# The split of the next job's weights, given a place 300 instructions earlier in the scheduler's order

## The chip, the cores and the metric

The kernel runs on one core of one Trainium2 chip. The metric is the device time of one execution in microseconds (us), the median of several executions. The engines are named as the profile names them: PE is the matrix engine (PEld its weight loads), DVE the vector engine, ACT the scalar engine, POOL the gather and scatter engine, SP the engine that only issues transfers. Each engine works through its own list of instructions in order. An instruction whose input is not there yet holds up everything behind it on its engine.

## The reference, cut to what matters

One layer of a graph network on 1250 nodes of width 1024 with 20000 edges, sorted by target, of 8 types. The part that the change touches is the relational convolution and the projections beside it:

```python
xn = _layernorm(x)
out = xn @ root + bias
for r in range(8):
    mask = (edge_type == r)
    sums = segment_sum(xn[src] * mask[:, None], dst)
    cnt = segment_sum(mask, dst)
    out = out + (sums / maximum(cnt, 1)[:, None]) @ weight[r]
z = concatenate([out, xn]) @ w_gate + b_gate
h = tanh(out) * z + xn * (1 - z)
```

Beside it stand a linear attention over all nodes (projections `w_q`, `w_kv`, `w_out`) and, after both, a gated feed-forward layer whose operands are rounded to a 4-bit grid in blocks of 16. All data is float32.

## The kernel before

**Products first, messages after.** The kernel turns the order of the convolution round: it first multiplies all nodes by the weight of each type (`y_d`, 8 x 1250 rows, in two halves of 512 columns) and then adds up, for each target, the rows of `y_d` that its edges name, each times 1/count. Three products are made in plain float32 in the front part of the program (`plain`). The remaining 18 are **jobs** of the function `product`, numbered 0 to 17 here: jobs 0 to 4 are the rest of the first half (types 3 to 7), jobs 5 to 12 the second half of all 8 types, job 13 the q, k and v projections (384 columns), jobs 14 and 15 the root product, jobs 16 and 17 the half of the gate that acts on `xn`.

**A job.** A job multiplies ten blocks of 128 nodes by one 1024 x 512 weight matrix, in float32 made of three faster products of split operands. The nodes' split operands (`xH`, `xL`, `xD`) are resident. The weights are split by `limb(job, k)`, lines 476 to 491, for each of the eight slices k of 128 rows: SP loads the slice (`raw`, three buffers), DVE masks it (`h`, L487, two buffers), ACT copies the mask as `wH` (L488), DVE makes `wL` (L489) and `wD` (L490). That is one load, one ACT and three DVE instructions. The three results live in the pool `wl`, which has 26 places: 24 for the eight slices of the running job and two over. Hence the split of the next job can't go far ahead; most of it has to wait until the last block of the running job has used a slice. Therefore `product` calls `more(k)` only within its last piece: after the last block's matmuls of slice k (L529 to L531) it traces the next job's slice k + 1.

A job has nine pieces: blocks 0 and 1 together (48 matmuls), then one block at a time (24 matmuls each). After a piece, ACT and DVE take the sums out of PSUM (L537, L538, and L545 where there is a bias line), and ACT issues the store (L546). After that comes the job's share of other work, called `beside`: in jobs 0 to 4 the rounding of the feed-forward weights (`ffn_rows`), in jobs 5 to 12 about 20 messages each, in jobs 13 to 17 28 messages each.

**A message** is a tile of 128 edges, for one half of the columns: there are 157 for each half, 314 in all. POOL gathers 128 rows of `y_d` into `msg` (L444, four buffers); two messages later DVE makes a 0/1 matrix `sel` (L453), ACT `hi` (L455) and DVE the remainder in `msg` (L457), PE multiplies twice (L460, L461) into one of two PSUM tiles, ACT copies the sums out (L462) and issues their store to `seg_d` (L463). The messages of the second half (numbers 157 to 313 here) can't start before job 12 has stored its last block, since they gather from what jobs 5 to 12 write. 140 of them are spread over jobs 13 to 17; the last 17 come after the jobs.

**After the jobs** follow the sums for the attention (`mix_sums`, `mix_pairs`), the closing of segments that cross tiles (`open_segments`, lines 764 to 779, the second call after the last message), the numerators of the attention for blocks 0 to 4 (`mix_num`) with the transposes of the feed-forward weights between them (`ffn_weight`, L157), and then ten blocks of the gate, the output and the feed-forward layer, which PE paces.

**What sets the order.** The program is traced from top to bottom. The tile framework then schedules it on a simulated machine: whenever an engine is free there, it takes, of the instructions whose inputs and buffers are ready, the one with the lowest number. The number is the place in tracing order. The order found that way is fixed in the program, and the chip's engines follow it whatever happens there. `tc.high_priority(n)` lowers the numbers of what is traced inside it by n, and the numbering goes on as before when it is left.

Of the kernel before, what the change touches and what calls it, by code (L numbers as in the profile page):

```python
# [26 lines left out]
H, DH = 8, 16  # L27
FIRST = 5
LAG = 2
EARLY = 140  # L30
PLAIN = 3
TOP = -4096
# [6 lines left out]
def block_rows(b):  # L39
    return slice(b * BR, min((b + 1) * BR, N))  # L40


def rows_of(b):
    return min(BR, N - b * BR)
# [3 lines left out]
def gps_layer(ctx: ExitStack, tc: tile.TileContext, x, src, dst, et, w_rel, w_root, bias,  # L48
# [393 lines left out]
    def gather(nh, t):  # L442
        msg = em.tile([128, HD], F32, name="msg")
        gathered_last[0] = G.indirect_dma_start(  # L444
            out=msg[:, :], out_offset=None, in_=y_d[nh][:, :],
            in_offset=bass.IndirectOffsetOnAxis(ap=key[:, t:t + 1], axis=0)).ins
        return lambda: segments(nh, t, msg)
# [28 lines left out]
    def limb(job, k):  # L476
        raw = rawp.tile([128, HD], F32, name="raw")
        if job is QKV:
            V.memset(raw[:, 384:], 0.0)
            nc.sync.dma_start(raw[:, :128], w_q[k * 128:(k + 1) * 128, :])  # L480
            nc.sync.dma_start(raw[:, 128:384], w_kv[k * 128:(k + 1) * 128, :])
            V.tensor_scalar(raw[:, :384], raw[:, :384], gm[:, k:k + 1], None, op0=ALU.mult)
        else:
            nc.sync.dma_start(raw, job[0][k * 128:(k + 1) * 128, :])
        h = topp.tile([128, HD], F32, name="h")
        Wh, Wl, Wd = (wl.tile([128, HD], F32R, name=f"w{c}", tag="w") for c in "HLD")
        V.tensor_scalar(h.bitcast(I32), raw.bitcast(I32), TOP, None, op0=ALU.bitwise_and)  # L487
        S.copy(Wh, h)  # L488
        V.tensor_tensor(Wl, raw, h, ALU.subtract)  # L489
        V.scalar_tensor_tensor(Wd, Wl.bitcast(F32), -1.0 / LOW, h, op0=ALU.mult, op1=ALU.add)  # L490
        return Wh, Wl, Wd

    psum_pools(ctx, sg=2)
    with ExitStack() as main:
# [5 lines left out]
        jobs = [(w_rel[r][:, cols[nh]], y_d[nh][r * N:(r + 1) * N, :], None)  # L500
                for nh, r in [(0, r) for r in range(PLAIN, R)] + [(1, r) for r in range(R)]]
        jobs += [QKV] + [(w[:, cols[nh]], d[:, cols[nh]], v[cols[nh]])
                         for w, d, v in ((w_root, root_d, bias), (w_gate[D:2 * D, :], gx_d, b_gate)) for nh in range(2)]
        held_of = [[] for _ in jobs]
        anchor = [None]

        def product(i, beside, from_=0, to_=9):


            job, held = jobs[i], held_of[i]  # L510
            _, dest, line = job
            n = dest.shape[1]
            if line is not None:
                rows_line = bias_p.tile([128, HD], F32, name="line")
                nc.sync.dma_start(rows_line, line[None, :].to_broadcast([128, HD]))

            def more(k):
                if i + 1 < len(jobs) and k < KC:
                    held_of[i + 1].append(limb(jobs[i + 1], k))

            def piece(blocks, last):
                ab = [[psum["ab"].tile([128, HD], F32, name="ab") for _ in range(2)] for _ in blocks]
                if last:
                    more(0)
                for k in range(KC):
                    Wh, Wl, Wd = held[k]
                    for (pa, pb), b in zip(ab, blocks):
                        ns, p = block_rows(b), rows_of(b)
                        T.matmul(pa[:p, :n], xH[:, k, ns], Wh[:, :n], start=(k == 0), stop=False)  # L529
                        T.matmul(pa[:p, :n], xL[:, k, ns], Wl[:, :n], start=False, stop=(k == KC - 1))  # L530
                        T.matmul(pb[:p, :n], xD[:, k, ns], Wd[:, :n], start=(k == 0), stop=(k == KC - 1))  # L531
                    if last:
                        more(k + 1)
                for (pa, pb), b in zip(ab, blocks):
                    p = rows_of(b)
                    yt = yp.tile([BR, HD], F32, name="yt")[:p]
                    S.mul(yt[:, :n], pa[:p, :n], 1.0 + LOW)  # L537
                    made = V.scalar_tensor_tensor(yt[:, :n], pb[:p, :n], -LOW, yt[:, :n], op0=ALU.mult, op1=ALU.add)  # L538
                    if i == R - PLAIN - 2:
                        anchor[0] = made.ins  # L540
                    if job is QKV:
                        V.tensor_scalar(yt[:, :128], yt[:, :128], rms[:p, b, 1:2], None, op0=ALU.mult)
                        V.tensor_scalar(yt[:, 128:n], yt[:, 128:n], rms[:p, b, 0:1], None, op0=ALU.mult)
                    if line is not None:
                        V.tensor_tensor(yt, yt, rows_line[:p], ALU.add)  # L545
                    S.dma_start(dest[block_rows(b), :], yt[:, :n])  # L546

            groups = [(0, 1)] + [(b,) for b in range(2, NB)]
            done = 0
            for j, g in enumerate(groups):  # L550
                piece(g, j == len(groups) - 1)
                while done < len(beside) and done * (to_ - from_) < len(beside) * (j + 1 - from_):
                    beside[done]()
                    done += 1
# [32 lines left out]
        def message(nh, t):  # L587

            if t < ST:
                waiting.append(gather(nh, t))  # L590
            if t >= LAG:
                waiting.pop(0)()

        def messages(nh, t0, t1):
            return [lambda t=t: message(nh, t) for t in range(t0, t1)]


        tiles = messages(0, 0, ST + LAG)
        for i in range(R):
            product(n0 + i, share(tiles, i, R))  # L600

        tiles = messages(1, 0, EARLY)
        for i in range(5):
# [63 lines left out]
    with ExitStack() as late:  # L667
# [26 lines left out]
        def mix_pairs(b):  # L694
            if b == 0:
                bd_ps.append(mm_tile())
            ps, n = bd_ps[0], rows_of(b)
            kks = []
            for c in range(4):
                kk = pb.tile([BR, 2, DH, DH], F32, name="kk")[:n]  # L700
                ck = kv[:n, b, c * 32:c * 32 + 32].rearrange("p (h i) -> p h i", h=2)
                cv = kv[:n, b, 128 + c * 32:128 + c * 32 + 32].rearrange("p (h e) -> p h e", h=2)
                V.tensor_tensor(kk, ck[:, :, None, :].to_broadcast([n, 2, DH, DH]),
                                cv[:, :, :, None].to_broadcast([n, 2, DH, DH]), ALU.mult)
                kks.append(kk.rearrange("p h e i -> p (h e i)"))
            for c, kk in enumerate(kks):
                T.matmul(ps[32 * c:32 * c + 32], kv[:n, b, 32 * c:32 * c + 32], kk,
                         start=(b == 0), stop=(b == NB - 1))
            if b == NB - 1:
                V.scalar_tensor_tensor(  # L710
                    bd.rearrange("p (h x) -> p h x", h=2), ps.rearrange("p (h x) -> p h x", h=2), 0.5,
                    mask2[:, :, None].to_broadcast([128, 2, 256]), op0=ALU.mult, op1=ALU.mult)
# [77 lines left out]
        rest += [lambda b=b: mix_pairs(b) for b in range(NB)]  # L790
        done = EARLY
        for i, p in enumerate(rest):
            p()
            while done < ST + LAG and (done - EARLY) * len(rest) < (i + 1) * (ST + LAG - EARLY):
                message(1, done)
# [137 lines left out]
```

## Time and profile before

| | us |
|---|---|
| median of 3 runs | 2024.85 (2014.6 to 2028.79) |
| the profiled execution | 2014.05 |
| its span in the trace | 2012.3 |
| front part, to the first matmul of job 0 | 298.2 |
| jobs 0 to 4 | 298.2 to 583.8 |
| jobs 5 to 12 | 583.8 to 1124.8 |
| jobs 13 to 17 | 1124.8 to 1502.1 |
| after the jobs, to the first transpose of the first output block | 1502.1 to 1652.1 |
| ten output blocks | 1652.1 to 2012.3 |

The limits of the stages are starts of instructions in the timeline: the first L529 of a job, and the first L157 on `u`. A job's matmul of 512 columns starts 0.23 us after the one before it when PE runs at full clock, although each is shown as 0.39 us long: matmuls overlap. So a block of 24 takes 5.6 us, and a gap is best read as the time between two starts beyond 0.23 us. Summed so over jobs 0 to 17, PE lost 81 us, of which 51 us in jobs 13 to 17. By job, start, length and time lost of the last ones:

| job | starts at | length | messages multiplied in it | lost | of it in the first piece | in the last piece |
|---|---|---|---|---|---|---|
| 10 | 919.3 | 66.9 | 20 | 1.9 | 1.6 | 0.0 |
| 11 | 986.2 | 67.9 | 20 | 2.9 | 2.1 | 0.0 |
| 12 | 1054.1 | 70.7 | 20 | 5.7 | 3.5 | 0.0 |
| 13 | 1124.8 | 55.4 | 17 | 4.5 | 0.0 | 0.1 |
| 14 | 1180.3 | 89.9 | 34 | 18.4 | 11.3 | 6.3 |
| 15 | 1270.2 | 80.5 | 28 | 11.8 | 3.0 | 8.1 |
| 16 | 1350.7 | 79.7 | 28 | 11.1 | 2.4 | 7.8 |
| 17 | 1430.5 | 71.9 | 24 | 5.5 | 3.3 | 0.2 |

### The profile page before, as it was taken

How to read it: one execution, taken by the hardware profiler on the slowest of the kernel's cores; microseconds unless marked ns; L12 is line 12 of the kernel's file. 1: busy time of each engine (PE TensorE's matmuls, PEld its weight loads, DVE VectorE, ACT ScalarE, POOL GpSimd, SP SyncE). 2: the span in 40 equal slices, each digit the busy share in tenths (PEclk: the TensorE clock that was granted, in tenths of full speed). 3: DMA queues.
4: the chain of work that ended last, by engine and by line, in shares of the span. 5: the costliest groups of instructions: out<-in, count | busy, mean ns of one | idle time of the engine just before them, and what ended most of it. 6: DMA issues, size and time to landing. Idle time of an engine off the chain costs nothing. (4 is left out here: it accounts for less than half of the span.)

```text
span 2012.3 us, 24046 instructions
## 1 busy us (share of the span) xinstructions
PE 1889.7 (94%) x7828; PEld 1281.7 (64%) x7828; DVE 1315.7 (65%) x2940; ACT 755.3 (38%) x1307; POOL 614.1 (31%) x588
## 2 busy tenths in 40 slices
PE   6999999999999999999999989999897689999998
PEld 3465547777777777777777877667663244454544
DVE  6989936776644565456545666666655677777665
ACT  6211321121224454545454455555553223132311
POOL 2012478885012333333332234333243310010000
PEclk8999999999999999999999989889998759999999
DMA  6245324444336677766776687787689532122100
GB/s 211 75 137 142 102 58 132 121 121 126 117 118 213 223 227 227 229 229 222 226 228 202 205 254 253 240 253 241 214 264 320 199 101 84 63 84 69 37 21 29
DMA packets 158868, 332.76 MB, mean 165 GB/s; under 512 B 26974, under 2 KB 35844, under 8 KB 158742
## 3 DMA queue, kind: packets, MB, share of 16 engines
q0 software_dynamic: 39168, 110.63, 21.1%
q10 hardware_dynamic: 76570, 141.23, 18.9%
q1 hardware_dynamic: 43004, 79.36, 12.6%
q8 instruction: 62, 1.02, 0.2%
q14 instruction: 64, 0.52, 0.1%
HBM read 184.42 MB, written 146.53 MB: 164 GB/s over the span
## 5 line engine op out<-in xcount | busy, mean ns | idle before, releaser
L529 PE MATMUL ab<-wH,xH 128*128 128x512 f32 (+2 forms) x1440 | 569.2, 395 | 2.3 <-ACT wH L488 2.3
L531 PE MATMUL ab<-wD,xD 128*128 128x512 f32 (+2 forms) x1440 | 562.9, 395 | 3.8 <-DVE wD L490 3.1
L530 PE MATMUL ab<-wL,xL 128*128 128x512 f32 (+2 forms) x1440 | 565.3, 393 | 0.0
L444 POOL DMA_INDIRECT msg<-y_d,key x314 | 329.5, 1049 | 677.4 <-PE sm L461 328.3
L457 DVE SCALAR_TENSOR_TENSOR msg<-msg,weight,hi 128x512 fp32r<-128x512 f32 x314 | 234.0, 749 | 145.3 <-ACT hi L455 142.5
L531 PEld LDWEIGHTS ab<-wD,xD 128*128 128x128 f32 (+1 forms) x1440 | 268.6, 187 | 76.9 <-DVE wD L490 12.8
L529 PEld LDWEIGHTS ab<-wH,xH 128*128 128x128 f32 (+1 forms) x1440 | 270.2, 188 | 64.8 <-ACT wH L488 4.1
L530 PEld LDWEIGHTS ab<-wL,xL 128*128 128x128 f32 (+1 forms) x1440 | 270.1, 188 | 64.4 <-DVE wL L489 0.4
L455 ACT ACTIVATE hi<-msg,weight 128x512 fp32r<-128x512 f32 x314 | 222.4, 721 | 87.9 <-DMA msg<-y_d,key 29.4
L462 ACT COPY seg<-sm 128x512 f32<-128x512 f32 x314 | 181.8, 584 | 193.0 <-PE sm L461 150.3
L388 PE MATMUL mm<-wt,xnT 128*128 128x512 f32 (+1 forms) x480 | 225.6, 611 | 5.1 <-DMA wt<-in_L_gnn_weight_dram 5.1
L370 POOL DMA_INDIRECT sort_d<-pay,row x160 | 208.5, 1303 | 60.2 <-issue 48.4
L537 ACT ACTIVATE yt<-ab 128x512 f32<-128x512 f32 (+2 forms) x180 | 106.0, 592 | 319.8 <-PE ab L530 308.0
L538 DVE SCALAR_TENSOR_TENSOR yt<-ab,yt 128x512 f32<-128x512 f32 (+2 forms) x180 | 121.5, 680 | 144.8 <-ACT yt L537 143.9
L460 PE MATMUL sm<-hi,sel 128*128 128x512 f32 x314 | 133.3, 429 | 33.4 <-ACT hi L455 28.7
L453 DVE TENSOR_SCALAR sel<-iota_n,last_row 128x128 fp32r<-128x128 f32 x314 | 89.0, 286 | 104.5 <-PE sm L461 104.2
L461 PE MATMUL sm<-msg,sel 128*128 128x512 f32 x314 | 136.0, 434 | 21.7 <-DVE msg L457 21.5
L849 PE MATMUL mm<-wg,uT 128*128 128x512 f32 (+1 forms) x320 | 141.7, 596 | 1.5 <-DVE mr L122 1.0
L388 PEld LDWEIGHTS mm<-wt,xnT 128*128 128x128 f32 (+1 forms) x480 | 85.7, 190 | 90.0 <-issue 82.5
L488 ACT CAST wH<-h 128x512 fp32r<-128x512 f32 x144 | 88.5, 621 | 126.2 <-DVE h L487 119.0
L489 DVE TENSOR_TENSOR wL<-raw,h 128x512 fp32r<-128x512 f32 x144 | 98.1, 682 | 31.9 <-PE mm L388 31.9
L849 PEld LDWEIGHTS mm<-wg,uT 128*128 128x128 f32 (+1 forms) x320 | 59.5, 189 | 75.2 <-issue 70.4
(267 smaller groups left out, 2042.8 us busy)
## 6 DMA issues: line engine op xcount, KB each, us to landing
seg_d<-seg ACTq DMA_DIRECT2D x314, 256.0 KB
y_d<-yt ACTq DMA_DIRECT2D x144, 256.0 KB
raw<-in_L_gnn_weight_dram SPq DMA_DIRECT2D x104, 256.0 KB
db<-in_dst_dram POOLq DMA_DIRECT2D x32, 305.2 KB, 3.9
xt<-in_x_dram SPq DMA_DIRECT2D x18, 512.0 KB
msg<-y_d,key POOLq DMA_INDIRECT x314, 4.7
lb<-lo_d POOLq DMA_DIRECT2D x32, 156.2 KB, 4.0
root_d<-yt ACTq DMA_DIRECT2D x18, 256.0 KB
```

What stands on the lines that cost most here:

```text
L370: st = G.indirect_dma_start(out=sort_d[:, :], out_offset=bass.IndirectOffsetOnAxis(ap=row[:, t:t + 1], axis=0), in_=pay[:, t, :], in_offse ...
L388: T.matmul(ps[:n], xnT[:, k, block_rows(b)], held[k], start=(k == 0), stop=(k == KC - 1))
L444: gathered_last[0] = G.indirect_dma_start(out=msg[:, :], out_offset=None, in_=y_d[nh][:, :], in_offset=bass.IndirectOffsetOnAxis(ap=key[:, ...
L455: S.mul(hi, msg, weight[:, t:t + 1])
L457: V.scalar_tensor_tensor(lo, msg, weight[:, t:t + 1], hi.bitcast(F32), op0=ALU.mult, op1=ALU.subtract)
L460: T.matmul(ps, sel, hi, start=True, stop=False)
L461: T.matmul(ps, sel, lo, start=False, stop=True)
L462: S.copy(seg, ps)
L529: T.matmul(pa[:p, :n], xH[:, k, ns], Wh[:, :n], start=(k == 0), stop=False)
L530: T.matmul(pa[:p, :n], xL[:, k, ns], Wl[:, :n], start=False, stop=(k == KC - 1))
L531: T.matmul(pb[:p, :n], xD[:, k, ns], Wd[:, :n], start=(k == 0), stop=(k == KC - 1))
L849: T.matmul(ps[:n], uT[:, k, :n], wg[:, k, cs], start=(k == 0), stop=(k == KC - 1))
```

## The change

The instructions that `limb` traces from within `more` get numbers lower by 300. Nothing is added or removed: the same loads, splits, matmuls and messages are there, on the same engines, with the same buffers. Only the order in which the scheduler chooses among ready instructions is different. The first job's split, traced outside `more`, keeps its numbers.

```diff
 LAG = 2
+AHEAD = 300
 EARLY = 140
...
             def more(k):
                 if i + 1 < len(jobs) and k < KC:
-                    held_of[i + 1].append(limb(jobs[i + 1], k))
+                    with tc.high_priority(AHEAD):
+                        held_of[i + 1].append(limb(jobs[i + 1], k))
```

## The prediction

> **What bounds the kernel now.** I read the page first, then the table of stretches, then single engines in order of time. The page says PE is busy nearly throughout, with one dip:
>
> ```profile
> PE 1889.7 (94%) x7828; PEld 1281.7 (64%) x7828; DVE 1315.7 (65%) x2940; ACT 755.3 (38%) x1307; POOL 614.1 (31%) x588
> ...
> PE   6999999999999999999999989999897689999998
> ...
> PEclk8999999999999999999999989889998759999999
> ```
>
> Each slice is 50.3 us; the dip in slices 30 to 32 is the stretch after the jobs. The split of the weights lies in slices 6 to 28, where PE shows 8 or 9: what can be gained there is at most the 81 us lost between starts. The table of stretches, at the end of job 15, shows where such loss sits:
>
> ```profile
> core 0: us, PE busy (x) PEld busy (x) DVE busy (x) ACT busy (x) POOL busy (x), PEclk, DMA share, GB/s
> ...
> 1341.00:1351.00 10.00, 5.69 (x10) 2.62 (x11) 6.08 (x13) 5.30 (x11) 3.78 (x4) 0.68 0.77 248
> 1351.00:1365.00 14.00, 13.87 (x52) 10.21 (x52) 12.41 (x24) 7.03 (x12) 1.47 (x1) 0.87 0.65 200
> 1365.00:1400.00 35.00, 35.00 (x150) 27.48 (x149) 21.60 (x42) 18.94 (x33) 15.08 (x14) 1.00 0.80 261
> ```
>
> For 10 us PE does only 10 matmuls, and neither DVE nor ACT is full. PE in order of time says why:
>
> ```profile
> 1342.83 0.49 PE L461 MATMUL sm<-msg,sel 128*128 128x512 f32 x1 [0.81 <-DVE msg L457]
> 1344.62 0.79 PE L460 MATMUL sm<-hi,sel 128*128 128x512 f32 x1 [1.30 <-ACT hi L455]
> 1345.41 0.79 PE L461 MATMUL sm<-msg,sel 128*128 128x512 f32 x1
> 1347.50 0.80 PE L460 MATMUL sm<-hi,sel 128*128 128x512 f32 x1 [1.30 <-ACT hi L455]
> ...
> 1350.13 0.80 PE L461 MATMUL sm<-msg,sel 128*128 128x512 f32 x1 [0.62 <-DVE msg L457]
> 1350.72 0.63 PE L529 MATMUL ab<-wH,xH 128*128 128x512 f32 x1
> ```
>
> The last block's matmuls are done at 1340.5, and the next job's first matmul (L529) starts at 1350.72. Between them PE has nothing but messages, each waiting for its own ACT and DVE steps. The next job's weights are not split: DVE's first L489 of the new job starts at 1350.0 though its place was free long before. From there DVE splits at a slice per 1.54 us (L490 at 1357.73, 1359.28, 1360.82, 1362.36), and now the messages stand still, as POOL shows:
>
> ```profile
> 1351.20 1.47 POOL L444 DMA_INDIRECT msg<-y_d,key  x1 [0.90 <-PE sm L461]
> 1367.27 0.94 POOL L444 DMA_INDIRECT msg<-y_d,key  x1 [14.60 <-PE ab L531]
> ```
>
> So a boundary has two parts in series: about 10 us of messages without product, then 14 us of splitting without messages. In jobs 5 to 11 the first part is missing: L490 starts 0.5 us into the last piece, and only 1.6 to 2.1 us are lost in the next first piece, before an L461 whose DVE step stands behind the splits.
>
> The difference is the backlog. Gather 157 starts at 1136.8, 12 us into job 13, which multiplies 17 of its 28 messages. At 3.1 messages per piece the 11 missing ones are 3.5 pieces of older numbers, and in the scheduler's order they come before the split.
>
> **What the Trainium skill says.** "TensorE: Matmul & The Clock Gate", section "What's actually happening", has PE's clock halved after an idle window of about 3.4 us and restored after a busy one. The trace agrees: from 1350.72 to 1354.6 the starts are 0.43 us apart, later 0.23. A stall thus costs some 2 us beyond itself. "DMA: Bandwidth & Descriptors", section "Issuing engines are not separate DMA queues", says that transfers from all queues interleave on the same 16 engines: gathers slow down beside bulk loads. That bears on the stretch after the jobs; there the DMA share is 0.98 to 1.03 from 1500 to 1540, and an ACT step of a message waits 7.2 us for its gather.
>
> **The change, part by part.** I add up against the profiled execution's 2014.05 us (span 2012.3 and 1.75 around it). Every instruction keeps its length: L487 0.42, L488 0.62, L489 and L490 0.68 us, and SP's loads 0.33 each to issue. All five move together.
>
> *How far 300 reaches.* A one-block piece of jobs 13 to 17 traces 24 matmuls, 3 or 4 output instructions and 3.1 messages of 8, some 53 instructions: 300 are 5.7 pieces. The split passes messages of about pieces 3 to 7 and remains behind older ones. In jobs 5 to 12 (45 per piece) 300 are 6.7 pieces.
>
> *Jobs 0 to 4.* The split passes the rounding of the feed-forward weights on DVE and its loads on SP. Job 1's first piece takes 14.8 us against 11.1 in jobs 2 and 4, job 3's 11.5: I take **-4**, ends 0 and -5. The rounded weights are read only after 1502, so their delay is covered.
>
> *Jobs 5 to 12.* The split is on time already. What PE waits for is a message behind the split, and that isn't cured by putting the split further ahead. I take **0**, ends -12 (1.5 us at each of 8 boundaries) and +12.
>
> *Jobs 13 to 17.* Removable is what was lost at the boundary beyond the 1.6 us of jobs 5 to 11. Into 14: 11.3 - 1.6 = 9.7. Into 15: 6.3 + 3.0 - 1.6 = 7.7. Into 16: 8.1 + 2.4 - 1.6 = 8.9. Into 17: 7.8 + 3.3 - 1.6 = 9.5. But a job without stalls is shorter, so fewer messages fit beside it. The backlog grows from 11 by about 5 per job, to 16, 21 and 26, or 3.5, 5, 7 and 8 pieces. At the last two boundaries part of it is older than 300 instructions, so the split waits again. I take the first two in full, the last two by half: 9.7 + 7.7 + 4.4 + 4.7 = **-26.5**, ends -15 and -34. With jobs 0 to 4 the jobs end 30 us earlier.
>
> *Messages.* What waits behind the split on DVE, ACT and SP is the messages, and for them POOL and PE. Each boundary stops them for about 14 us, as it did before (16 us by POOL's gaps), so the stop isn't new. But they have less time: before, 365 us from gather 157 to the end of the jobs, less 4 x 16 = 301 for 131 messages, 2.30 us each. Now 365 - 26.5 - 56 = 282 us, 123 messages. Eight more are left for the stretch after the jobs. There 26 took 85 us (1502.1 to 1587.7), 3.3 each beside the bulk loads. Eight at 2.3 to 3.3 are 18 to 26, I take **+22**. The last message ends at -30 + 22 = **-8**.
>
> *After the last message.* It was multiplied at 1587.7, and the first output block's transposes start at 1652.1, 64 us later. What the message itself forces is its store (1592.3 to 1598.3), the reload (4.5), the matmul (L774) at 1602.8 held by that reload, the addition into `seg_d` on POOL (issued 1609.3, 2.1, and landing), a gather (median 4.9 to land) and `u` (1.2): about 35 us, to 1623. The other 29 us are numerators and transposes that stood behind L774 on PE:
>
> ```profile
> 1592.46 1.12 PE L640 MATMUL mm<-bd,qT 32*128 32x512 f32 x2 [0.19 <-DVE prod L643]
> 1602.80 1.90 PE L774 MATMUL mm<-s,osel 29*29 29x512 f32 x2 [9.22 <-DMA s<-seg_d]
> 1604.63 2.81 PE L640 MATMUL mm<-bd,qT 32*128 32x512 f32 x6
> ```
>
> They don't depend on messages. With the jobs ended earlier and more messages to wait for, more of them should be scheduled between messages. I take two thirds, **-19**, ends 0 and -29. The output blocks keep their 360 us.
>
> Sum: -8 - 19 = -27, so 2014 becomes **1987** in a profiled execution. The median of the runs stands 0.5% above it (2024.85 to 2014.05, lowest 2014.6); I add half of that: **1992**. Best ends together: -5 - 12 - 34 + 22 - 29 = -58, or 1956. Worst: +12 - 15 + 40 (12 messages at 3.3) + 0 = +37, or 2051.
>
> **The rivals.**
>
> *The gain is handed back after the jobs (slower).* One mechanism: messages put off by the splits pile up until the jobs end and then run at 3.3 us each beside the bulk loads, while L774 still stands ahead of the numerators. For it: that price is measured, and PE is in order. Against it: POOL stands still for 14.6 us per boundary already. With 30 us gained and nothing overlapped it decides from 30 / 3.3 = 9 extra messages on. At 20 (5 for each of four boundaries) it gives +66 - 30 = +36, that is 2014 + 36 + 5 = 2055.
>
> *It hardly does what it says.* If the simulated backlog is deeper than 300 instructions, or a free place in `wl` rather than the number is what held L489 up, the boundaries stay. Against it: two of the 26 places are free throughout a job, and in job 12 the first L489 of the next job came 49 us before its last piece. Then only jobs 0 to 4 gain: 2014 - 4 + 5 = 2015.
>
> *The end is set by the messages alone.* The boundaries go, but every message keeps its time and nothing is overlapped: -8, or 2011.
>
> **How the numbers follow.** Forecast 0.66, handed back 0.17, no effect 0.10, messages alone 0.07. About 1% (20 us) is what a measurement of this kernel can tell from no change. Of the forecast's 0.66, 0.61 lie below 2004.6 and 0.05 above; 0.02 of the cases of no effect fall below as well: **faster 0.63**. Handed back with fewer than 17 extra messages (less than +26 us, by 3.3 each) stays within 1%: 0.04 of its 0.17, so **slower 0.13**. The rest, **same 0.24**. The range takes the forecast's ends and the milder half of the slower rival: **1952 to 2040**.
>
> **What will show it.** Right: job 14 and 15 at 75 us or less, from 89.9 and 80.5; the first L489 of a next job within 2 us of its last piece or ahead of it; PE's waits for ACT's `hi` in jobs 13 to 17 down from 13.9 us; PE in the jobs' end meeting L529 straight after the last block; more than 26 messages after the jobs; numerators (L640) before L774. Wrong: jobs 14 to 17 as long as before, a POOL gap over 20 us per boundary, over 35 messages after the jobs, or the stretch from the last message to the first output block still 64 us.

## The result and the profile after

The changed kernel takes 2038.85 us in the median of 20 runs (2024.69 to 2051.91), beside 2018.41 for the kernel before on the same chip (20 runs, 2010.65 to 2038.39): a ratio of 1.0092, 95% interval 1.0074 to 1.0111. So the change makes the kernel slower by 0.9%. The forecast was 1.6% faster.

The profiled execution of the changed kernel has a span of 2042.0 us, 29.7 more than that of before. The medians are 20.4 apart, so single stages of these two traces are exact only to some us. In what follows the stages are read from the traces and the sizes from the ratios. The line numbers of the changed kernel are higher by 1 up to `limb` and by 2 from `product` on: its L531 is L529 of before.

The page of the changed kernel, with the busy time and then PE and its granted clock in 40 slices of 51 us:

```profile
PE 1897.5 (93%) x7828; PEld 1292.0 (63%) x7828; DVE 1321.1 (65%) x2940; ACT 756.7 (37%) x1307; POOL 610.9 (30%) x588
...
PE   6999999989999999999999989898897689999998
...
PEclk9999999999999999999999999999997759999999
```

PE is nearly as busy as before, on a longer span; the dip after the jobs (slices 30 to 32) is still there. The rest is found by stages, by the same starts of instructions as in the table of before:

| | before | after | difference |
|---|---|---|---|
| front part | 298.2 | 295.5 | -2.7 |
| jobs 0 to 4 | 285.6 | 292.1 | +6.5 |
| jobs 5 to 12 | 541.1 | 554.3 | +13.2 |
| jobs 13 to 17 | 377.2 | 384.0 | +6.8 |
| after the jobs, to the first output block | 150.1 | 153.0 | +2.9 |
| ten output blocks | 360.2 | 363.2 | +3.0 |
| messages multiplied after the jobs | 27 | 27 | 0 |

In these two traces all three groups of jobs lose, the middle one most. For jobs 13 to 17 and for what follows them the differences are no larger than those between kernels that don't differ there (the ten output blocks took 359.9 to 364.2 us over all the kernels of this document). Over jobs 0 to 17 the time lost between PE's starts grows from 81 to 107 us.

**The boundary into job 16 again.** Changed kernel, PE in order of time (start, length, engine, line, operation; in brackets the idle time before it and what ended it):

```profile
1361.57 0.40 PE L461 MATMUL sm<-hi,sel 128*128 128x512 f32 x1
...
1364.70 0.50 PE L531 MATMUL ab<-wH,xH 128*128 128x512 f32 x1 [2.51 <-ACT yt L539]
1365.04 0.43 PE L532 MATMUL ab<-wL,xL 128*128 128x512 f32 x1
```

The table of stretches of the changed kernel, just before and just after that start:

```profile
1352.00:1364.70 12.70, 10.20 (x44) 7.04 (x42) 9.43 (x17) 7.33 (x14) 3.58 (x4) 1.00 0.76 249
1364.70:1380.00 15.30, 15.07 (x57) 11.71 (x57) 13.06 (x27) 6.81 (x12) 4.63 (x4) 0.89 0.60 194
```

Before, 10 us with 10 matmuls lay between the last block and the next job; now the last block's matmuls go on to 1361.80, and job 16 starts 2.9 us later (the 44 matmuls of the first line are nearly all the last two blocks'). The split now goes ahead as it was meant to: DVE makes the third result (L491) of job 16's first slice at 1356.10, 8.6 us before the job's first matmul, where before the change even the second (L489) came only 0.7 us before it. But the first matmul waits none the less, and no longer for the weights: it waits for ACT's L539, the step that takes an older block's sums out of PSUM. ACT and then DVE show what stands ahead of that step:

```profile
1363.54 0.62 ACT L489 CAST wH<-h 128x512 fp32r<-128x512 f32 x1 [1.64 <-DVE h L488]
1364.06 1.08 ACT L539 ACTIVATE yt<-ab 128x512 f32<-128x512 f32 x2
```

```profile
1363.02 0.43 DVE L488 TENSOR_SCALAR h<-raw 128x512 int32<-128x512 int32 x1 [1.86 <-DMA raw<-in_L_gnn_w_gate_dram]
```

The first of the two L539 belongs to block 7, whose last matmul started at 1347.41. In between ACT did messages' steps and four `wH` of the split (1356.33, 1358.54, 1360.04, 1363.54), the last of them only when DVE had got a slice that was late. So the split, put ahead, has also passed the running job's own results. POOL shows that the messages still stand during the split:

```profile
1358.29 0.94 POOL L445 DMA_INDIRECT msg<-y_d,key  x1 [3.04 <-PE ab L532]
1372.13 1.62 POOL L445 DMA_INDIRECT msg<-y_d,key  x1 [12.90 <-PE ab L532]
```

**What PE waits for in jobs 13 to 17.** The table of waits has: engine, tile and line, what was waited for, then us in total, times, longest. Kernel before:

```profile
PE sm L460 <- ACT hi L455: 13.9, 9, 2.5
PE sm L461 <- DVE msg L457: 4.9, 10, 0.8
```

Changed kernel:

```profile
PE ab L531 <- ACT yt L539: 13.4, 5, 4.0
PE sm L461 <- ACT hi L456: 6.5, 9, 2.3
PE sm L462 <- DVE msg L458: 6.0, 13, 0.8
```

The wait for a message's `hi` is halved. In its place stands a wait of nearly the same total, 13.4 us, for a free PSUM tile `ab`, five times. Two of them are the first matmuls of job 14 (3.95 us, at 1201.81) and job 16 (2.51 us); at both, ACT's last step ahead of L539 is a `wH` whose slice was late (ACT stood 2.93 and 1.64 us). At the other three (6.9 us together) it is the copy of a message's sums (L463). Job 14 became shorter (79.1 us, from 89.9), jobs 15 and 17 longer (83.8 and 81.5, from 80.5 and 71.9).

**Jobs 5 to 12.** The same view of PE shows one wait that grew, from DVE's last step of a message (before, first fence) to its first step (after, second fence):

```profile
PE sm L461 <- DVE msg L457: 12.1, 8, 1.9
```

```profile
PE sm L461 <- DVE sel L454: 20.3, 7, 3.2
```

This is one stall per boundary, of up to 3.2 us. All of PE's waits there grew from 14.4 to 23.0 us. After each of six of these stalls PE also ran at half clock for 3.4 us; before, that happened twice. The stretch of the changed kernel from 665.5 on (columns as above):

```profile
665.50:668.90 3.40, 3.40 (x8) 2.75 (x9) 2.77 (x6) 1.31 (x2) 0.94 (x1) 0.50 0.28 96
```

At half clock starts are 0.43 us apart instead of 0.23, so such a stretch costs some 1.6 us. An estimate from these figures is 8.6 us of waits and four more such stretches, 15 us, beside the 13.2 measured. What DVE does there, changed kernel, around the start of job 6 at 655.03:

```profile
653.95 0.68 DVE L490 TENSOR_TENSOR wL<-raw,h 128x512 fp32r<-128x512 f32 x1
657.34 0.43 DVE L488 TENSOR_SCALAR h<-raw 128x512 int32<-128x512 int32 x1 [2.71 <-DMA raw<-in_L_gnn_weight_dram]
...
664.53 0.68 DVE L491 SCALAR_TENSOR_TENSOR wD<-wL,h 128x512 fp32r<-128x512 f32 x1
665.13 0.28 DVE L454 TENSOR_SCALAR sel<-iota_n,last_row 128x128 fp32r<-128x128 f32 x1
```

DVE stands 2.71 us at a split step whose slice has not landed. SP issued that slice's load at 651.45, so it took 5.9 us from issue to use. It is slice 4, counted from 0, and in every one of jobs 6 to 12 DVE stands there longest: 2.4 to 3.3 us, where before it stood 1.3 to 2.5 us. All the rest of the split comes before the 0.28 us step `sel` at 665.13, and PE resumes with L461 at 665.47 after a gap of 2.87 us.

**After the last message**, changed kernel, PE:

```profile
1612.56 0.40 PE L462 MATMUL sm<-msg,sel 128*128 128x512 f32 x1
1613.08 1.72 PE L642 MATMUL mm<-bd,qT 32*128 32x512 f32 x6
...
1629.45 1.90 PE L776 MATMUL mm<-s,osel 29*29 29x512 f32 x2 [10.44 <-DMA s<-seg_d]
1631.28 2.81 PE L642 MATMUL mm<-bd,qT 32*128 32x512 f32 x6
...
1678.78 1.94 PE L158 MATMUL tr<-ident,u 128*128 128x128 f32 x8 [2.48 <-issue]
```

Nothing has moved: from the last message to the first output block it is 66.2 us (64.4 before), and PE again waits for the reload (10.44 us, 9.22 before) with the numerators (L642) behind it.

### The profile page after: what moved, and what is told of

Its sections match the earlier page's. It is cut to its first block, busy times and chain, and to the rows that moved or that the text cites. A ratio compares the mean times of both kernels' runs of the same rounds, so it can differ in the third digit from the quotient of the medians.

```text
span 2042.0 us, 24167 instructions
## 1 busy us (share of the span) xinstructions
PE 1897.5 (93%) x7828; PEld 1292.0 (63%) x7828; DVE 1321.1 (65%) x2940; ACT 756.7 (37%) x1307; POOL 610.9 (30%) x588
## 4 chain that ended last, share of the span: by engine, by line
PE 68%; DMA 12%; issue 10%; DVE 7%; ACT 2%; POOL 1%; SPq 0%; ACTq 0%; DVEq 0%; POOLq 0%
PE ab L531 11%; PE ab L533 11%; PE ab L532 11%; PE mm L389 9%; PE mm L851 7%; PE mm L876 5%; DMA raw<-in_L_gnn_weight_dram 3%; PE sm L461 3%; DMA msg<-y_d,key 3%; PE mm L892 3%; PE sm L462 3%; DMA seg_d<-seg 2%; PE tr L158 1%; PE sm L335 1%; DVE wD L491 1%
## 5 line engine op out<-in xcount | busy, mean ns | idle before, releaser
L531 PE MATMUL ab<-wH,xH 128*128 128x512 f32 (+2 forms) x1440 | 573.7, 399 | 16.2 <-ACT yt L539 13.4
L531 PEld LDWEIGHTS ab<-wH,xH 128*128 128x128 f32 (+1 forms) x1440 | 272.2, 189 | 83.2 <-ACT yt L539 15.3
L463 ACT COPY seg<-sm 128x512 f32<-128x512 f32 x314 | 181.8, 583 | 168.9 <-PE sm L462 105.6
L539 ACT ACTIVATE yt<-ab 128x512 f32<-128x512 f32 (+2 forms) x180 | 105.8, 589 | 330.8 <-PE ab L532 281.3
L461 PE MATMUL sm<-hi,sel 128*128 128x512 f32 x314 | 134.3, 432 | 45.1 <-DVE sel L454 20.3
L489 ACT CAST wH<-h 128x512 fp32r<-128x512 f32 x144 | 89.2, 620 | 148.4 <-DVE h L488 116.5
L461 PEld LDWEIGHTS sm<-hi,sel 128*128 128x128 f32 x314 | 61.3, 195 | 82.5 <-ACT hi L456 26.5
```

The costliest lines, as they stand in the source:

```text
L461: T.matmul(ps, sel, hi, start=True, stop=False)
L463: S.copy(seg, ps)
```

## The experiments

Ratios are to the kernel before, run on the same chip in turn, with the 95% interval. "Jobs 5 to 12" and the like are stages of the profiled execution. With the split where it was, jobs 5 to 12 took 539.7 to 547.3 us in seven kernels that don't differ there, and jobs 13 to 17 took 376.4 to 383.9 in seven whose late jobs are those of before: a difference of some 5 us in one trace says little. Kernels with few runs (4 to 5 of e1_mid, of the two without loads and of the three with four places) have the widest intervals.

### The change in parts

```diff
-                    with tc.high_priority(AHEAD):
+                    with tc.high_priority(AHEAD) if 5 <= i <= 12 else ExitStack():
```

In e1_mid the split is ahead at the boundaries of jobs 5 to 12, in e1_late at those of jobs 13 to 16 (`13 <= i <= 17`), in e1_first at those of jobs 0 to 4.

> The split is put ahead only at the eight boundaries traced in jobs 5 to 12; everything else keeps its numbers. Theory A (in jobs 5 to 12 the split passes a message's DVE steps, DVE then waits in order for the split's own loads, and PE waits for that message): jobs 5 to 12 take about 554 us from start to start (541 before), PE waits some 20 us for L454's sel there, and the kernel is 8 to 16 us slower than before. Theory R (the rival of the prediction: messages put off come back at 3.3 us each after the jobs): messages aren't behind in these jobs, so jobs 5 to 12 stay within 3 us of 541 and the kernel within 5 us of before.

> The split is put ahead only at the four boundaries of jobs 13 to 16. Theory B (there the jobs can't run ahead of the messages, because their results leave PSUM by ACT and DVE behind older messages, so the stretch is paced by the messages and the split's place only moves the stall): jobs 13 to 17 take 370 to 385 us (377 before), 27 messages are left for after the jobs, the kernel is within 8 us of before. Theory R: the jobs end earlier, more than 35 messages are left, and the kernel is over 15 us slower than before. The prediction's own mechanism: jobs 13 to 17 take about 350 us and the kernel is 20 us or more faster.

> The split is put ahead by 300 at the boundaries of jobs 0 to 4 alone. Theory (the parts add up: 1.0067 for jobs 5 to 12 and 1.0021 for jobs 13 to 16 of the 1.0092 of the whole change, so that 0.0004 is left): within 3 us of before, with jobs 0 to 4 at 284 to 289 us; the 6.5 us that these jobs lost in the profiled execution of the whole change came from where their results waited in that one execution. Rival (the loss is in the order itself): jobs 0 to 4 at 291 us or more and a time 4 to 7 us above before.

| | ratio | interval | its own jobs | of before |
|---|---|---|---|---|
| e1_first | 1.0025 | 1.0011 to 1.0039 | 293.8 | 285.6 |
| e1_mid | 1.0067 | 1.0042 to 1.0092 | 550.8 | 541.1 |
| e1_late | 1.0021 | 1.0008 to 1.0034 | 380.8 | 377.2 |

No part gains. Two thirds of the loss is in jobs 5 to 12; the parts add up to 1.0113, the whole was 1.0092. For e1_first the rival was right, the loss is in the order: job 2 takes 63.7 us, as in the whole change (63.6), against 55.7 before. Its trace, of the slowest of its 20 runs, shows what happens. DVE at 411, between steps of the split:

```profile
405.93 0.69 DVE L540 SCALAR_TENSOR_TENSOR yt<-ab,yt 128x512 f32<-128x512 f32 x1 [0.79 <-ACT yt L539]
411.03 0.69 DVE L137 TENSOR_REDUCE q_sc<-fw 128x32 f32<-128x512 f32 x1 [4.42 <-DMA fw<-in_L_ffn_w_up_dram]
```

and ACT, which makes `wH` behind DVE's `h`:

```profile
418.04 0.62 ACT L489 CAST wH<-h 128x512 fp32r<-128x512 f32 x1 [5.86 <-DVE h L488]
...
422.31 0.59 ACT L539 ACTIVATE yt<-ab 98x512 f32<-98x512 f32 x1
```

DVE waits 4.42 us for a slice of the feed-forward weights. Behind it stand the steps that round that slice and then the split, behind the split's `h` stands ACT, and behind ACT's `wH` steps the step L539 that would free a PSUM tile; PE stands 5.18 us. It is the chain seen ahead of job 16, there with a slice of the split itself. It is read from the trace; no run took it apart.

### Jobs 5 to 12: which step of DVE holds the message up

e4_sel_mid is e1_mid with `sel` traced ahead by 600:

```diff
-        V.tensor_scalar(sel, iota_n[:, :128], last_row[:, t:t + 1], None, op0=ALU.is_equal)
+        with tc.high_priority(600):
+            V.tensor_scalar(sel, iota_n[:, :128], last_row[:, t:t + 1], None, op0=ALU.is_equal)
```

> As the run with the split ahead only in jobs 5 to 12, but each message's sel (one DVE instruction of 0.28 us) gets a number lower by 600, so it isn't put behind the split. Theory A: PE's wait of about 20 us for sel in jobs 5 to 12 goes below 3 us; what is left is the wait for the message's next DVE step (L458), as before (12 us), and jobs 5 to 12 take 540 to 548 us instead of 554. If not the place behind the split but the later splits themselves cost the time, jobs 5 to 12 stay at 552 or more.

Ratio 1.005 (1.0029 to 1.007), jobs 5 to 12 547.7 us. PE's table of waits in e4_sel_mid:

```profile
PE sm L463 <- DVE msg L459: 17.9, 7, 3.0
```

The wait for `sel` is gone and comes back at the next DVE step of the same message. So it isn't the place of `sel` that costs: DVE as a whole is late there. What little e4_sel_mid may win over e1_mid lies within the intervals.

e2_noload_mid leaves seven of eight weight loads of jobs 6 to 12 out and splits the first slice again; e2_noload_b does so with the split where it was.

```diff
-    def limb(job, k):
-        raw = rawp.tile([128, HD], F32, name="raw")
-        if job is QKV:
+    def limb(job, k, once=None):
+        raw = once[0] if once else rawp.tile([128, HD], F32, name="raw")
+        if once:
+            pass
+        elif job is QKV:
...
```

> The split is put ahead by 300 at the boundaries of jobs 5 to 12 alone, and jobs 6 to 12 split the first slice that they loaded for every k: seven of eight of their weight loads are left out, so the output is not the reference's, while every split, matmul and message stays. Theory A (DVE works in order and stands at a split whose slice has not landed, with the selection and the rounding of the next message behind it): PE's waits for DVE's sel and msg at these boundaries fall from 23 us with the loads to under 8, jobs 6 to 11 take 67.5 us or less each (69.5 to 70 with the loads) and jobs 5 to 12 together at most 541, about 10 us less than with the loads. Theory B (the mere place of the twenty steps of the split ahead of the message's, each of full length, is the cost): the waits stay near 20 us and jobs 5 to 12 near 550.

> The same loads left out (output not the reference's), with the split where it was before. Theory A: in the old order the splits come late enough for their loads, so that little is won: jobs 5 to 12 within 4 us of the 541 of before, and the new order without loads no longer slower than this. Theory B: also about 541, but 8 us or more below the new order without loads. If the loads' bytes themselves disturbed the messages, both kernels without loads would be faster than before by 8 us or more in these jobs.

| | ratio | interval | jobs 5 to 12 | DVE's waits for `raw` there |
|---|---|---|---|---|
| before | 1 | | 541.1 | 15.2 |
| e1_mid | 1.0067 | 1.0042 to 1.0092 | 550.8 | 22.1 |
| e2_noload_b | 0.9924 | 0.9901 to 0.9946 | 525.1 | none |
| e2_noload_mid | 0.9946 | 0.9929 to 0.9963 | 524.9 | none |

Without the loads both orders take the same, 525 us, and PE's waits for DVE's `sel` and `msg` are gone from the list. So by these traces the loads are in jobs 5 to 12 the whole cost of the new order; and they cost the old order too, 16 us. DVE's waits for them, 15.2 and 22.1 us, grow with that cost (16 and 26 us) but needn't equal it: PE's half-clock stretches come on top, and there is one such stretch left in each kernel without loads. I had expected little from leaving them out in the old order: that was missed.

### Four places for slices

A load can only be issued once the split three slices back has given its place free. e8_raw4_b gives the old order a fourth place, and takes one of the 26 for split weights for it; e8_raw4_mid does the same with the split ahead in jobs 5 to 12, e8_raw4_all with the whole change. e8_wl25_b, the control, takes the place for split weights away and gives no place for slices.

```diff
-    rawp = late_r.enter_context(tc.tile_pool(name="rawp", bufs=3, side="right"))
+    rawp = late_r.enter_context(tc.tile_pool(name="rawp", bufs=4, side="right"))
...
-        wl = main.enter_context(tc.tile_pool(name="wl", bufs=26))
+        wl = main.enter_context(tc.tile_pool(name="wl", bufs=25))
```

> The order of before, with four places for loaded slices in place of three, paid for with one of the 26 places for split weights (25 are left). Theory A (a slice's load can only be issued when the split three slices back is done, and lands 4 to 6 us later, against 1.54 us per split): the fourth place takes most of the waits in jobs 5 to 12, which fall from 541 to 532 or less (525 is what no loads gave), and the whole is 6 to 12 us shorter than before. Rival (the place taken from the split weights stops the split sooner and takes it back, or the load is late for the bytes on the DMA engines, not for its issue): jobs 5 to 12 stay at 538 to 548.

> The same four places for loaded slices, with the split put ahead at the boundaries of jobs 5 to 12. Theory A: the cost of the new order shrinks with the waits for loads: jobs 5 to 12 at 532 to 540 instead of the 551 of the same order with three places. If the new order costs something that is not the load (steps of a message pushed back), it stays 9 us or more above the old order with four places.

> The whole change (ahead by 300 in all jobs) with four places for loaded slices and 25 for split weights. Theory (in jobs 5 to 12 the loads of the slices are the cost; in jobs 0 to 4 it is another load, that of the feed-forward weights, which the fourth place doesn't touch; in jobs 13 to 17 little is won or lost): jobs 5 to 12 at 528 to 534 us, jobs 0 to 4 at 288 to 295, the whole at 2003 to 2013, which is 4 to 14 us above the old order with the same places and still faster than before by 7 to 17. Rival (with the loads out of the way, being ahead pays): 1998 or less. Rival (the order costs beside the loads): 2014 or more.

> The order of before with 25 places for split weights in place of 26, and three for slices as before: the control. Theory A (the fourth place for slices is what helps): within 5 us of before, jobs 5 to 12 at 538 to 546. Rival (25 places hold the split back and so help by themselves): 2008 or less.

| | median | ratio | interval | jobs 5 to 12 |
|---|---|---|---|---|
| e8_raw4_b | 1998.84 | 0.9899 | 0.9865 to 0.9933 | 524.9 |
| e8_raw4_mid | 2002.7 | 0.9915 | 0.9886 to 0.9944 | 529.6 |
| e8_raw4_all | 2003.14 | 0.9889 | 0.9849 to 0.993 | 530.4 |
| e8_wl25_b | 2014.33 | 0.997 | 0.9956 to 0.9983 | 537.0 |

DVE's waits for `raw` in jobs 5 to 12 tell the same. Kernel before:

```profile
DVE h L487 <- DMA raw<-in_L_gnn_weight_dram: 15.2, 12, 2.5
```

Changed kernel:

```profile
DVE h L488 <- DMA raw<-in_L_gnn_weight_dram: 21.2, 12, 3.3
```

The split ahead with four places (e8_raw4_mid):

```profile
DVE h L488 <- DMA raw<-in_L_gnn_weight_dram: 5.5, 7, 1.4
```

In e8_raw4_b no such wait is left, and its jobs 5 to 12 take what they take without any load. Theory A holds: the time hung on how early a load could be issued, not on its bytes.

The traces give the sizes. In the new order three places leave two splits, 3.2 us, between a load's issue and the moment when DVE wants it; the loads of slice 4 took 5.6 to 6.4 us. Four places leave three splits, 4.6 us; the loads that DVE then waited for (slice 5, but for one) took 5.0 to 6.4 us. So a fourth place shortens the stop and doesn't quite end it.

The control won 0.3% by itself (on another chip), so some seven tenths of e8_raw4_b's 1.0% belong to the fourth place. With four places the whole change neither costs nor gains anything that these few runs can tell (0.9889 beside 0.9899, four runs each, on different chips, intervals overlapping by far). The traces still have jobs 5 to 12 some 5 us longer with the split ahead (529.6 and 530.4 beside 524.9), and DVE's waits of 5.5 us go with that.

For e8_raw4_all I had expected 288 to 295 us in jobs 0 to 4; they took 281.1, so the stop in job 2 isn't bound to the new order alone. Why it is absent there was not followed further. All three kernels with four places beat both the kernel before and the changed one.

### Jobs 13 to 17: what holds a job back

e3_out_late puts the split ahead in jobs 13 to 17, and with it the results, from PSUM to the store. e3_out_late_b puts the results ahead alone.

```diff
+                    with tc.high_priority(OUT) if i >= n0 + R else ExitStack():
                     yt = yp.tile([BR, HD], F32, name="yt")[:p]
...
                     S.dma_start(dest[block_rows(b), :], yt[:, :n])
```

(OUT is 400; the lines between are indented with it.)

> As the run with the split ahead only in jobs 13 to 16, and in jobs 13 to 17 also ACT's and DVE's steps that take results out of PSUM and their store get numbers lower by 400. Theory B: the product is now free of the messages: PE's waits for ACT's yt (13.4 us in the changed kernel) vanish, jobs 14 to 17 take 75 us or less each, jobs 13 to 17 together under 355, and more than 35 messages are left for after the jobs. If the product was held by something else (the weights, the messages' own matmuls), jobs 13 to 17 stay above 370. The end: 10 to 30 us faster than before if the numerators fill the time of the messages that are left, within 10 us of before if each costs 3.3 us there.

> Only the results of jobs 13 to 17 (the steps from PSUM to the store) are put ahead by 400; the split stays where it was. Theory B of the late jobs (what holds these jobs is that their results leave PSUM behind older messages; the place of the split is the smaller part): jobs 13 to 17 take 340 to 360 us, and more than 36 messages are left after them. Rival (the two have to come together, because a late split stops a job whatever its results do): jobs 13 to 17 stay at 370 to 380 with 27 to 30 messages left. Either way the whole time is within 10 us of before, since what the jobs win comes back after them.

| | ratio | interval | jobs 13 to 17 | messages left | last message after the jobs | to the first block |
|---|---|---|---|---|---|---|
| before | 1 | | 377.2 | 27 | 85.3 | 150.1 |
| e1_late | 1.0021 | 1.0008 to 1.0034 | 380.8 | 27 | 85.8 | 149.1 |
| e3_out_late_b | 1.0003 | 0.9988 to 1.0017 | 373.7 | 29 | 84.7 | 151.1 |
| e3_out_late | 1.0035 | 1.0016 to 1.0054 | 337.2 | 45 | 128.9 | 196.1 |

Only both together free the jobs: 40 us shorter, and PE's waits for the step that empties `ab` are gone from its list. Each alone does nothing. But the jobs then leave 18 messages more, the last message comes 43.6 us later after the jobs (2.4 us for each of the 18), and the stretch after the jobs is 46 us longer. What was won is handed back in full. Since the results were put ahead of the split as well as of the messages, these runs don't tell which of the two mattered more. The fourth place bears on it: in e8_raw4_all PE's waits for the step that empties `ab` fall from 13.4 to 5.0 us in these jobs, but they take 377.9 us all the same, and 373.8 in e8_raw4_b. Here late slices are not the whole of it.

### After the jobs: can the rest be laid beside the messages?

e6_pairs_out is e3_out_late with the pair products traced ahead of the opening steps of rows and segments, which share PSUM tiles with the messages:

```diff
-        rest = [mix_sums, open_rows, lambda: open_segments(0)]
+        rest = [mix_sums]
         rest += [lambda b=b: mix_pairs(b) for b in range(NB)]
+        rest += [open_rows, lambda: open_segments(0)]
```

> The split and the results of jobs 13 to 17 are put ahead as before, and the pair products of the attention part (mix_pairs) are written out ahead of the rows' and segments' opening steps. Theory (they wait for a PSUM tile that the opening steps and the messages share, so they can run while the 45 messages left do): the stretch after the jobs falls from 196 to 170 us or less and the whole is 2000 or less. Rival (the stretch is set by the messages alone, each gather in turn, and by what follows the last of them): it stays at 190 to 200 us, the last message 125 to 130 us after the jobs, the whole 2015 to 2025.

Ratio 1.0026 (1.0008 to 1.0044); 194.4 us to the first block. The rival was right.

e14_b leaves the jobs as before and moves the numerators between the messages:

```diff
-        rest += [lambda b=b: mix_pairs(b) for b in range(NB)]
+        rest += [lambda b=b: mix_ahead(b) for b in range(NB)]
...
-        open_segments(1)
...
         for b in range(FIRST):
-            mix_num(b)
+            with tc.high_priority(600):
+                mix_num(b)
...
+        open_segments(1)
```

(`mix_ahead` is `mix_pairs` under `tc.high_priority(600)`.)

> The order of before in the jobs; after them the pair products and the numerators of the first five blocks are put ahead by 600, and the second segments' opening steps, whose PSUM tiles stand before the numerators' in the ring of four, are written out after the numerators. Theory (numerators stood behind the last message for two reasons, the ring and the order, and nothing else): 12 or more of their matmuls run before the last message, the stretch from the last message to the first output block falls from 64 us to 35 to 48, and the whole is 8 to 25 us shorter than before. Rival (DVE and PE have as much to do either way, so that the messages end later by what is saved): the last message comes 95 us or more after the jobs in place of 85, and the whole is within 6 us of before.

The order came out as meant: in the trace, 40 records of numerator matmuls stand before the last matmul of the second closing, 10 before. The stretch from the last message, counted here from its first matmul, to the first block fell from 64.8 to 42.4 us. But the last message came 111.4 us after the jobs instead of 85.3, and the sum is 153.8 instead of 150.1; ratio 1.0031 (1.0015 to 1.0047). One stretch of e14_b's trace shows why, PE in order of time:

```profile
1589.64 2.09 PE L641 MATMUL mm<-bd,qT 32*128 32x512 f32 x8
1592.49 1.25 PE L648 MATMUL mm<-rl,qT 128*128 128x264 f32 x2 [0.77 <-DVE prod L644]
...
1594.55 1.20 PE L461 MATMUL sm<-hi,sel 128*128 128x512 f32 x2
```

In the 5 us of a block of numerators no message is multiplied. The theory was right about what held the numerators and wrong about its worth: in this stretch PE and DVE work them off one after the other with the messages. It isn't shown that this is all: from 1566 to 1614 the granted clock was 0.62, against 0.88 in the last 43 us of messages before, and no run separates the two.

## Why the prediction was wrong, by its steps

**Jobs 0 to 4, -4.** It came out as +6.5 in the trace, and a ratio of 1.0025 (5 us) when done alone. The step took it that the feed-forward rounding could be passed without harm. It is passed only in part: in e1_first a step of it, waiting 4.42 us for its own load, stands among the split's, and the running job's results stand behind both. That is read from the trace; with four places for slices the stop was absent.

**Jobs 5 to 12, 0.** This is the largest failure: +13.2 in the trace, +0.67% alone (13.5 us), above the upper end of +12. "The split is on time already" was read from PE alone. DVE's own list of waits had the line with 15.2 us for `raw` in it, and the prediction didn't read it. Each of DVE's stops at a slice that has not landed holds up whatever stands behind it. With the split ahead that stop became longer: DVE stood at slice 4 for 2.4 to 3.3 us in each of jobs 6 to 12 instead of 1.3 to 2.5, PE waited longer for the message behind, and its clock was halved more often. That more of the message now stands behind the split is true too, but e4_sel_mid shows that freeing `sel` alone doesn't help. The prediction's sentence that a message behind the split isn't cured by putting it further ahead was right, and the next thought, that it is made worse, was left out. The Trainium skill, "DMA: Bandwidth & Descriptors", section "Latency and other measured facts", speaks of a fixed cost of about 2 us for a DMA. A whole slice of 256 KB beside gathers and stores took longer here, at job 6 4.5 us (before) and 5.9 us (after) from issue to use. At 1.54 us per slice, the two splits that three places allow in between are too short for either.

**Jobs 13 to 17, -26.5.** It came out as +6.8 in the trace and +0.21% alone (4 us). The mechanism at the boundary was right: the split went ahead, the wait for `hi` fell from 13.9 to 6.5 us, and POOL's gaps at the four boundaries were 11.9 to 15.0 us (14.6 to 15.5 at three of them before). The step that failed is "removable is what was lost at the boundary". A piece needs its PSUM tiles, these come free through ACT and DVE, and there the job's results stand behind messages and, at the first matmuls of jobs 14 and 16, behind the split itself, which stood at a late slice. The stall moved from the weights to `ab`, 13.4 us. The sentence "What waits behind the split on DVE, ACT and SP is the messages" left out the running job's own results: the prediction followed what the split was meant to pass, not what else it passes and what the job needs next.

**Messages, +22.** No message more was left: 27 in both (the prediction counted 26 before). A job that can't run ahead of its messages leaves no more of them behind. The price of a message left was 2.4 us in e3_out_late, in the 2.3 to 3.3 stated.

**After the last message, -19.** It came out as +1.8 us. The jobs did not end earlier, so nothing could move; but e14_b shows that moving them would have gained nothing anyhow. Of the 64 us, 22 can be moved ahead of the last message, and it then comes 26 us later. That work doesn't depend on what is waited for is not enough to hide it: the engines that do it have to be free.

**The rivals.** "The gain is handed back" described e3_out_late exactly, with 18 extra messages, but not the change itself, which had no gain to hand back. "It hardly does what it says" gave 2015 and named the free place in `wl` as the limit; the order did change, so that was not it. No rival had the mechanism that decided, a stop of DVE at a load. The range, 1952 to 2040, just holds the measured 2038.85, but by luck: its upper end was meant for messages handed back.

## What to carry to other kernels

Before work is put ahead on an engine that goes in order, read that engine's own waits, not only those of the engine that paces the kernel: what is put ahead brings its waits for loads with it, and everything that it has passed, the running job's own results included, stands behind them. If the loads are late, give them another place to land before anything is moved: here one buffer was worth 1.0%, together with the place it took, and the order nothing that the runs could tell. And for a job to run ahead of other work, its inputs and the way out of its results must both be ahead; then count what is left for later.

## What the runs showed of the hardware

The same load of 256 KB, slice 4 of a job's weights, took 4.3 to 5.4 us from issue to use in the old order (jobs 6 to 12; DVE was waiting for it each time) and 5.6 to 6.4 us in the new one; what made it longer was not tried. And 25 places for split weights in place of 26 made the kernel 0.3% faster, where I had expected no difference; that was not followed up either.

PE's clock was halved without any long stop. The kernel before, around the boundary into job 16:

```profile
1341.10:1344.50 3.40, 1.23 (x3) 0.48 (x3) 2.60 (x6) 2.23 (x4) 1.85 (x2) 1.00 0.75 231
1344.50:1354.80 10.30, 8.13 (x15) 4.51 (x16) 6.55 (x12) 5.82 (x11) 3.40 (x4) 0.50 0.84 262
```

The second line has a granted clock of 0.50. In the 3.4 us ahead of it PE was busy for 1.23 us, and its longest idle time there was 1.30 us. The prediction put the halving down to an idle window of about 3.4 us; in this trace a stretch of that length with short gaps in it was enough.
